# A list schedule that counts TensorE's instructions, and layer-3 parts added on VectorE and GpSimd

## The chip, the cores and the metric

The kernel runs on one core of a Trainium2 chip. The metric is the device time of one execution in microseconds (us), lower is better; the time of a kernel is the median of its runs. Besides its times each kernel has one profiled execution, with a page that sums it up and a trace that can be asked for groups of instructions, waits, the clock that TensorE was granted, and the order in time.

The engines are called PE (TensorE's matrix products; PEld is its loading of weights), DVE (VectorE), ACT (ScalarE), POOL (GpSimd) and SP (SyncE, which only issues DMAs here).

## The reference: what is computed

A decoder of four layers on 32 sequences of 64 tokens, that is 2048 tokens of 256 float32 numbers. Every layer adds three things to the residual `x`: an attention, a cross-attention to a context of 64 vectors of 128 numbers, and a feed-forward part. Each works on the layer norm of `x`.

```python
x = x + _L0_attn_ref(_layernorm(x, axis=-1), ...)
x = x + _L0_xattn_ref(_layernorm(x, axis=-1), ctx_1024, mask_BxS2_bf1, ...)
x = x + _L0_ffn_ref(_layernorm(x, axis=-1), ...)
...
x = x + _L3_ffn_ref(_layernorm(x, axis=-1), ...)
return x
```

Two places matter here. Layer 0's attention has 32 query heads of 64 numbers, 8 key heads, rotary positions and a causal mask: many score products of 64 by 64. Layer 3's feed-forward sends each token to the best 6 of 64 experts (each takes at most 128 tokens), multiplies what the expert returns by the token's weight and adds the six:

```python
h_r = jax.nn.silu(g_r) * v_r
out_r = jnp.einsum('ech,ehd->ecd', h_r, w_down)
y_ts = out_r[flat_e, pos_c]
y_ts = jnp.where(valid[:, None], y_ts, 0.0)
routed = (y_ts.reshape(N, TOPK, C) * w[:, :, None]).sum(axis=1)
```

## The kernel before

**Tiles and stages.** The tokens are 16 tiles of 128; the residual of each, `self.X[i]`, stays in SBUF. `GROUPS = (8, 6, 2)`: the tiles go through the network in three groups. `body` (L2569) writes down the later, narrow stages of one group together with the early, wide stages of the next; `weave` (L2557) takes steps from two such streams by their stated shares.

**Recording.** No engine is called directly. `Recorder` (L380) keeps every operation as an `Op` with the engines that may do it, the views that it reads and writes, and the operations that must come before it. `combine` gives an elementwise operation to DVE or POOL, `either` to DVE or ACT; with `quick` set, as it is for the last stretch of the kernel, `combine` leaves DVE alone.

**Planning.** `in_turns` (L773) makes a list schedule. `Order.run` (L613) keeps a clock for every engine and goes on taking the operation with the lowest key among those whose predecessors are planned: the key is the time at which it could start, with additions. `duration` (L467) says how long each operation is held to take. On TensorE a product's key is raised by `SWITCH` (0.1) when its `part` of the 128x128 array (how many rows and columns it uses, in steps of 32, 64 and 128) is not that of the product before. A tile's buffer is one of a few slots of its tag; it becomes free, by the plan, when the last operation that uses the tile is done. `fill` (L589) puts products without use (`spare`, L874) where PE would wait over 1.6 us. `elsewhere` (L602) leaves an operation to another engine when that one would be done with it sooner. After a plan, `backwards` and `renumber` (L727) turn the list round, with the planned ends as its new order, and plan again: nine plans in all, of which every other one, in the forward direction, may be kept; the shortest by its own clock is. `issue` (L2480) then emits the operations in that order, so nearly every instruction of the profile has line L2504. They are told apart by the tiles they write and read.

**Layer 0's scores.** For one tile `unit_L0_attn` (L1022) makes 128 products of 32 rows (the half of a head, for the rotary positions) by 64 columns by 64, recorded so that the row strip `j` changes after every two:

```python
for half in range(2):
    for j in range(4):
        r = slice(32 * j, 32 * j + 32)
        for x in range(2):
            nc.tensor.matmul(sc[j][64 * x : 64 * x + 64, col],
                qs[hi][r, gp, half, b, x], kk[r, half, hi, b], start=(half == 0), stop=(half == 1))
```

**The end of the kernel.** For the first 14 tiles layer 3's experts work on slots of tokens: `unit_L3_experts` (L2416) makes the products of four experts, weighs the rows, and scatters them with 64 indirect DMAs on POOL's queue into a tensor `parts` in device memory, six rows for each token. `unit_L3_parts` (L2462) loads them again for each tile, in two DMAs of four and two rows a token, adds them and writes the result out. PE sums the first four with the identity as weights, DVE adds the two others and both sums to `x`. The last two tiles use all experts densely instead (`unit_L3_dense`, L2384) in the same stretch of time.

Of the kernel before, what the change touches and what calls it, by code (L numbers as in the profile page):

```python
# [23 lines left out]
ALU = mybir.AluOpType  # L24
# [204 lines left out]
class Tile:  # L229
    def __init__(self, tag, shape, dtype, name, pool):  # L230
        self.tag, self.shape, self.dtype, self.name, self.pool = tag, shape, dtype, name, pool
        self.psum = pool == "psum"
        self.writes, self.reads = [], []
        self.left, self.first, self.last = 0, None, None
        self.slot = self.real = None


class View:
# [282 lines left out]
NEAR = 10  # L521


def combines(op, engine, method):

    if engine == "gpsimd":
        return method == "tensor_tensor" and ALU.pow not in op.args
    return engine == "vector" and not any(v.t.psum for v in op.outs + op.ins if isinstance(v, View))


class Order:
    ENGINES = ("tensor", "vector", "scalar", "gpsimd", "sync")

    def __init__(self, ops, slots, horizon, spare):
        self.ops, self.slots, self.horizon, self.spare = ops, slots, horizon, spare
        self.free_at = {e: 0.0 for e in self.ENGINES}
        self.table, self.moved = 0, 0.0
        self.part = None

        self.until = {"vector": 0.0, "gpsimd": 0.0}  # L540

        self.free = {tag: [(0.0, k) for k in range(n)] for tag, n in slots.items()}

        events = {tag: [] for tag in slots}
        for o in ops:
            for t in o.tiles:
                if t.tag in slots and t.first == o.at:
                    events[t.tag].append((o.at, 0, t))
                if t.tag in slots and t.last == o.at:
                    events[t.tag].append((o.at, 1, t))  # L550
        self.events = {tag: sorted(ev, key=lambda e: e[:2]) for tag, ev in events.items()}

        work, self.pos = 0.0, []
        for o in ops:
            self.pos.append(work)
            if o.ways[0][0] == "tensor":
                work += duration("tensor", o.ways[0][1], o.args, o.kw)
# [55 lines left out]
    def run(self):  # L613
# [6 lines left out]
        for o in self.ops:  # L620
            if o.waits == 0:
                enter(o)
        done, oldest, result, self.ends = [False] * len(self.ops), 0, [], {}
        while not all(done[oldest:]):
            limit = self.pos[oldest] + self.horizon
            best = None
            for e in self.ENGINES:
                now, seen, first = self.free_at[e], 0, 1e9
                for o in ready[e]:
                    if self.pos[o.at] > limit or seen == 32:  # L630
                        break
                    seen += 1
                    since = o.ready
                    opens = [t for t in o.tiles if t.slot is None and t.tag in self.slots]
                    if opens:
                        if any(not self.free[t.tag] for t in opens):
                            continue
                        since = max([since] + [self.free[t.tag][0][0] for t in opens])
                    start = max(now, since)
                    method = next(m for w, m in o.ways if w == e)  # L640
                    cost = duration(e, method, o.args, o.kw)
                    key = max(now, o.soft, since)
                    if e == "tensor":
                        if start == now:
                            first = min(first, self.pos[o.at])
                        if part(method, o.args) != self.part:
                            key += SWITCH
                            cost += SWITCH
                        elif self.pos[o.at] > first + NEAR:
                            key += SWITCH  # L650
                        elif self.part != (128, 128):
                            key = start
                    if e == "scalar":
                        table = TABLES.get(getattr(o.args[2], "name", "") if method == "activation" else "", 0)
                        if table and table != self.table:
                            key += 1.3
                            cost += 1.3
                    if e == "vector" and self.until["gpsimd"] > start and combines(o, e, method):
                        cost += min((1 - BESIDE) * (self.until["gpsimd"] - start), cost / BESIDE - cost)
                    if len(o.ways) > 1 and self.elsewhere(o, e, since, start + cost):  # L660
                        continue
                    if best is not None and (key, o.at) >= best[0] and not (
                        o is best[1] and start + cost < best[3] + best[4]
                    ):
                        continue
                    if opens and not self.may_open(o):
                        continue
                    best = ((key, o.at), o, e, start, cost, opens)
                    if key <= now:
                        break  # L670
            assert best is not None, "nothing can go on"
            _, o, e, start, cost, opens = best
            filler = self.fill(o, start) if e == "tensor" else None
            if filler:
                o, start, opens = filler, self.free_at[e], []
# [20 lines left out]
                table = TABLES.get(getattr(o.args[2], "name", "") if m == "activation" else "", 0)  # L696
                self.table = table or self.table
            if e == "tensor":
                self.part = part(o.ways[0][1], o.args)
            lat = latency(e, o)  # L700
            if o.ways[0][1] in DMA:
                v = next(v for v in o.outs + o.ins if isinstance(v, View) and v.dtype != I32)
# [1 line left out]
                lat = 2.0 + self.moved - got  # L704
            for t in o.tiles:
                t.left -= 1
                if t.left == 0 and t.tag in self.slots:
                    bisect.insort(self.free[t.tag], (got + lat, t.slot))
            for n in o.after:
                same = len(n.ways) == 1 and n.ways[0][0] == e and o.ways[0][1] not in DMA  # L710
                at = (start if e in ("tensor", "sync") else got + 0.03) if same else got + lat
# [3 lines left out]
                if n.waits == 0:  # L715
                    enter(n)
            if not filler:
                done[o.at], self.ends[o] = True, got
            while oldest < len(done) and done[oldest]:
                oldest += 1  # L720
            oldest = min(oldest, len(done) - 1)
# [2 lines left out]
        return result  # L724


def renumber(ops, ends):  # L727

    waits, late = {o: 0 for o in ops}, []
    for o in ops:  # L730
        for n in o.after:
            waits[n] += 1
    count = len(ops)
    for at, o in enumerate(ops):
        if waits[o] == 0:
            heapq.heappush(late, (-ends[o], at, o))
    ops.clear()
    while late:
        o = heapq.heappop(late)[2]
        o.at = len(ops)  # L740
        ops.append(o)
        for n in o.after:
            waits[n] -= 1
            if waits[n] == 0:
                count += 1
                heapq.heappush(late, (-ends[n], count, n))


def rewind(ops):

    for o in ops:
        o.waits, o.ready, o.soft = 0, 0.0, 0.0
        for t in o.tiles:
            t.slot, t.left, t.first, t.last = None, 0, None, None
    for o in ops:
        for n in o.after:
            n.waits += 1
        for t in o.tiles:
            t.left += 1
            t.first, t.last = o.at if t.first is None else t.first, o.at  # L760
# [12 lines left out]
def in_turns(ops, slots, horizon, spare, rounds):  # L773

    best, ops = None, list(ops)
    for k in range(2 * rounds + 1):
        plan = Order(ops, slots, horizon, spare)
        result = plan.run()
        if k % 2 == 0 and (best is None or plan.length < best[0]):
            best = plan.length, result, {t: t.slot for o, _ in result for t in o.tiles}  # L780
        if k < 2 * rounds:
            backwards(ops)
            renumber(ops, plan.ends)
            rewind(ops)
    for t, slot in best[2].items():
        t.slot = slot
    return best[1]


class Net:  # L790
# [1671 lines left out]
    def unit_L3_parts(self, i):  # L2462
        nc = self.nc
        z = [self.b4(4, 256), self.b2(2, 256)]
        for a, (k, m) in enumerate(((0, 4), (4, 2))):
            self.load(
                z[a],
                self.parts(
                    of=lambda x, k=k, m=m: x.rearrange("(t k) n -> t k n", k=6)[i * P : (i + 1) * P, k : k + m, :]
                ),  # L2470
            )
        ps = self.mm()[:, :256]
        self.prod(ps, [(self.k("ident"), z[0][:, k, :]) for k in range(4)])
        nc.combine(z[1][:, 0, :], z[1][:, 0, :], z[1][:, 1, :], ALU.add)
        nc.vector.tensor_tensor(self.X[i], self.X[i], z[1][:, 0, :], ALU.add)
        self.outproj(i, ps)
        nc.sync.dma_start(out=self.out[i * P : (i + 1) * P, :], in_=self.X[i])


# [133 lines left out]
```

## Time and profile before

| | |
|---|---|
| times of three runs | 2928.95, 2929.83, 2934.93 us; median 2929.83 |
| profiled execution | 2933.83 us, span of its instructions 2932.0 us |
| mean granted clock of TensorE | 0.977 |
| PE busy | 2861.3 us, 98% of the span, 28774 records |
| DVE, ACT, POOL busy | 71%, 47%, 49% |
| DMA | 259.22 MB, mean 88 GB/s |
| first parts load, end of the last output | 2881.4 us, 2932 us |

Instructions are called records in the trace. A float32 product is two records of PE, each with a weight load of its own; a transpose is one. The duration of a PE record reaches to the modelled end of its way through the array, which overlaps with the next, so what a product costs in a row of products is the distance of starts. In the lines of groups, "32*64" are the rows and columns of the array that are used, then come what is written, the count, the busy time, the mean duration in ns, and the idle time of the engine before these instructions with what ended it. "issue" means that the engine waited for nothing that the profile shows. In the lines of windows, each engine has its busy time and number of instructions, and after them stand the granted clock (1.00 is full speed), the share of the DMA engines and GB/s.

### The profile page before, as it was taken

How to read it: one execution, taken by the hardware profiler on the slowest of the kernel's cores; microseconds unless marked ns; L12 is line 12 of the kernel's file. 1: busy time of each engine (PE TensorE's matmuls, PEld its weight loads, DVE VectorE, ACT ScalarE, POOL GpSimd, SP SyncE). 2: the span in 40 equal slices, each digit the busy share in tenths (PEclk: the TensorE clock that was granted, in tenths of full speed). 3: DMA queues.
4: the chain of work that ended last, by engine and by line, in shares of the span. 5: the costliest groups of instructions: out<-in, count | busy, mean ns of one | idle time of the engine just before them, and what ended most of it. 6: DMA issues, size and time to landing. Idle time of an engine off the chain costs nothing.

```text
span 2932.0 us, 70600 instructions
## 1 busy us (share of the span) xinstructions
PE 2861.3 (98%) x28774; PEld 2388.2 (81%) x28774; DVE 2080.8 (71%) x5093; ACT 1390.0 (47%) x2637; POOL 1449.5 (49%) x1294
## 2 busy tenths in 40 slices
PE   9999999999999999999999999999999999998899
PEld 8888888777788889888888788878897878877678
DVE  5564447677566656676689997787757889888864
ACT  1223225555544233454466575665335665457360
POOL 4552233223656443423667446677534477357462
PEclk8999999999999899999999999999999999999999
DMA  4002331300161135312100110112473131211245
GB/s 175 22 10 100 117 123 54 142 1 30 62 275 46 59 132 160 124 41 66 55 30 20 44 59 13 45 35 80 134 276 141 57 121 59 75 60 41 89 152 210
DMA packets 120327, 259.22 MB, mean 88 GB/s; under 512 B 27077, under 2 KB 81880, under 8 KB 107588
## 3 DMA queue, kind: packets, MB, share of 16 engines
q1 hardware_dynamic: 110212, 230.61, 22.5%
q0 software_dynamic: 9792, 24.10, 2.4%
q8 instruction: 228, 3.74, 0.5%
q14 instruction: 95, 0.78, 0.1%
HBM read 179.31 MB, written 78.77 MB: 88 GB/s over the span
## 4 chain that ended last, share of the span: by engine, by line
PE 88%; DVE 7%; ACT 2%; POOL 2%; issue 1%; DMA 0%; DVEq 0%; SPq 0%; ACTq 0%; POOLq 0%
PE L_xattn_mm L2504 13%; PE ssm_heads_mm L2504 11%; PE L_attn_mm L2504 10%; PE pair_mm L2504 10%; PE cross_out_mm L2504 9%; PE L_ffn_mm L2504 5%; PE rope_mm L2504 5%; PE L_block_mm L2504 4%; PE turn_mm L2504 3%; PE cross_scores_mm L2504 2%; PE L_dense_mm L2504 2%; PE heads_mm L2504 2%; PE small_scores_mm L2504 1%; PE L_experts_mm L2504 1%; PE norm_mm L2504 1%
## 5 line engine op out<-in xcount | busy, mean ns | idle before, releaser
L2504 PE MATMUL pair_mm<-norm_b,load_ssm_w 128*128 128x256 f32 x1280 | 311.2, 385 | 2.8 <-DVE ssm_heads_b L2504 2.6
L2504 PEld LDWEIGHTS pair_mm<-norm_b,load_ssm_w 128*128 128x128 f32 x1280 | 237.8, 192 | 44.5 <-issue 12.9
L2504 POOL TENSOR_TENSOR L_xattn_sm<-L_xattn_sm,__init___consts 128x8 f32<-128x8 f32 (+2 forms) x64 | 188.2, 2945 | 57.3 <-DVE L_xattn_sm L2504 56.6
L2504 ACT ACT_TABLE_LOAD x154 | 197.6, 1283 | 29.0 <-DVE ssm_heads_b L2504 12.4
L2504 DVE SCALAR_TENSOR_TENSOR ssm_heads_b<-pair_mm,load_ssm_wp,ssm_heads_b 128x248 f32<-128x248 f32 (+2 forms) x480 | 194.3, 465 | 13.3 <-ACT ssm_heads_b L2504 12.5
L2504 POOL TENSOR_TENSOR norm_sm<-norm_sm,__init___consts 128x1 f32<-128x1 f32 (+1 forms) x149 | 95.3, 644 | 199.5 <-DVE norm_sm L2504 184.0
L2504 ACT COPY L_xattn_b<-L_xattn_mm 128x512 f32<-128x512 f32 x176 | 103.1, 591 | 174.3 <-PE L_xattn_mm L2504 160.0
L2504 ACT COPY turn_b<-turn_mm 128x512 f32<-128x512 f32 x203 | 110.7, 593 | 135.5 <-PE turn_mm L2504 134.3
L2504 PE MATMUL rope_mm<-norm_b,load_L_attn_w 128*128 128x128 f32 x1280 | 165.1, 282 | 0.3 <-ACT norm_b L2504 0.2
L2504 PEld LDWEIGHTS rope_mm<-norm_b,load_L_attn_w 128*128 128x128 f32 x1280 | 157.0, 197 | 9.7 <-issue 6.3
L2504 PE MATMUL ssm_heads_mm<-load_ssm_w,ssm_heads_b 128*128 128x256 f32 x640 | 163.5, 385 | 1.3 <-ACT ssm_heads_b L2504 0.8
L2504 ACT COPY norm_b<-norm_mm 128x256 f32<-128x256 f32 (+1 forms) x138 | 58.0, 431 | 189.4 <-PE norm_mm L2504 164.2
L2504 POOL TENSOR_TENSOR L_attn_b<-rope_b 128x256 f32<-128x256 f32 x151 | 109.6, 747 | 71.5 <-DVE rope_b L2504 58.9
L2504 PEld LDWEIGHTS ssm_heads_mm<-load_ssm_w,ssm_heads_b 128*128 128x128 f32 x640 | 115.6, 190 | 32.4 <-issue 18.8
L2504 POOL TENSOR_TENSOR ssm_heads_b<-ssm_heads_b,ssm_heads_b 128x1024 f32<-128x1024 f32 x32 | 76.4, 2387 | 125.5 <-DVE ssm_heads_b L2504 60.9
L2504 DVE TENSOR_TENSOR rope_b<-rope_mm,__init___consts 128x512 f32<-128x512 f32 x160 | 103.2, 680 | 48.0 <-PE rope_mm L2504 37.8
L2504 POOL TENSOR_TENSOR heads_b<-heads_b,heads_sm 128x1024 f32<-128x1024 f32 x53 | 102.1, 1940 | 69.8 <-DVE heads_sm L2504 62.8
L2504 DVE TENSOR_SCALAR norm_b<-__init___x,norm_sm,norm_sm 128x256 f32<-128x256 f32 x192 | 115.8, 620 | 22.7 <-POOL norm_sm L2504 13.4
L2504 PEld LDWEIGHTS L_xattn_mm<-norm_b,load_L_xattn_w 128*128 128x128 f32 x1024 | 119.8, 192 | 7.9 <-issue 4.9
L2504 PE MATMUL L_attn_mm<-load_L_attn_w,L_attn_b 128*128 128x256 f32 x512 | 124.8, 391 | 0.0
L2504 PE MATMUL L_xattn_mm<-norm_b,load_L_xattn_w 128*128 128x128 f32 x1024 | 123.9, 276 | 0.0
L2504 PE MATMUL cross_out_mm<-load_L_xattn_w,cross_out_b 128*128 128x256 f32 x512 | 123.2, 387 | 0.0
(428 smaller groups left out, 7700.5 us busy)
## 6 DMA issues: line engine op xcount, KB each, us to landing
L_block_w<-in_f_rows SPq DMA_DIRECT2D x42, 770.0 KB
queue<-far_w SPq DMA_DIRECT2D x14, 1024.0 KB
load_ssm_w<-in_s_in SPq DMA_DIRECT2D x12, 1024.0 KB
parts<-far_w SPq DMA_DIRECT2D x10, 1024.0 KB
slots<-far_w SPq DMA_DIRECT2D x16, 548.0 KB
L_experts_b<-slots SPq DMA_DIRECT2D x32, 274.0 KB
units_L_xattn_w<-kept_x SPq DMA_DIRECT2D x8, 1024.0 KB
L_parts_b<-parts SPq DMA_DIRECT2D x14, 512.0 KB
```

The costliest lines, as they stand in the source:

```text
L2504: done = getattr(getattr(nc, e), method)(*map(real, op.args), **kw)
```

## The change

On TensorE the planner now keeps a stock of instructions. `STOCK`, `RATE` and `LOW` are 300 instructions, 85 a us, and 150. A product takes 4 from the stock, a transpose 2, and 85 come back in each planned us up to 300. A product that is shorter than its instructions take to come (under 47 ns for 4) gets a higher key when the stock is under 150, by the time that is missing to 150; so a large product that can start is taken first. When the stock doesn't reach for a product, its start is put off. Three smaller things change in the planner: a slot becomes free at the latest end of all operations on its tile, and not at the end of the one that is planned last; when nothing can be chosen, a second try ignores `elsewhere`; `renumber` orders by planned starts and by place in the plan, not by ends. In layer 3's parts PE has no product any more: four additions, each for DVE or POOL as the planner decides, sum the six rows of a token and add them to `x`.

```diff
@@ class Tile
+        self.until = 0.0
@@
+STOCK, RATE, LOW = 300.0, 85.0, 150.0
@@ class Order, __init__
+        self.stock, self.at = STOCK, 0.0
@@ Order.run
-        done, oldest, result, self.ends = [False] * len(self.ops), 0, [], {}
+        stuck, done, oldest, result, self.starts = False, [False] * len(self.ops), 0, [], {}
...
                         elif self.part != (128, 128):
                             key = start
+                        n = 2 if method == "transpose" else 4
+                        stock = min(STOCK, self.stock + (start - self.at) * RATE)
+                        if n > duration(e, method, o.args, o.kw) * RATE:
+                            key += max(0.0, LOW - stock) / RATE
+                        start += max(0.0, n - stock) / RATE
...
-                    if len(o.ways) > 1 and self.elsewhere(o, e, since, start + cost):
+                    if len(o.ways) > 1 and not stuck and self.elsewhere(o, e, since, start + cost):
                         continue
...
+            if best is None and not stuck:
+                stuck = True
+                continue
             assert best is not None, "nothing can go on"
+            stuck = False
...
             if e == "tensor":
-                self.part = part(o.ways[0][1], o.args)
+                self.part, n = part(o.ways[0][1], o.args), 2 if m == "transpose" else 4
+                self.stock, self.at = min(STOCK, self.stock + (start - self.at) * RATE) - n, start
...
+                t.until = max(t.until, got + lat)
                 if t.left == 0 and t.tag in self.slots:
-                    bisect.insort(self.free[t.tag], (got + lat, t.slot))
+                    bisect.insort(self.free[t.tag], (t.until, t.slot))
...
-                done[o.at], self.ends[o] = True, got
+                done[o.at], self.starts[o] = True, (start, len(result))
@@ renumber
-def renumber(ops, ends):
+def renumber(ops, starts):
...
+    key = lambda o: (-starts[o][0], -starts[o][1], o)
...
-            heapq.heappush(late, (-ends[o], at, o))
+            heapq.heappush(late, key(o))
@@ unit_L3_parts
+        add = lambda *v: nc.add([("vector", "tensor_tensor"), ("gpsimd", "tensor_tensor")], (*v, ALU.add), {})
...
-        ps = self.mm()[:, :256]
-        self.prod(ps, [(self.k("ident"), z[0][:, k, :]) for k in range(4)])
-        nc.combine(z[1][:, 0, :], z[1][:, 0, :], z[1][:, 1, :], ALU.add)
-        nc.vector.tensor_tensor(self.X[i], self.X[i], z[1][:, 0, :], ALU.add)
-        self.outproj(i, ps)
+        add(z[0][:, :2], z[0][:, :2], z[0][:, 2:])
+        add(z[1], z[1], z[0][:, :2])
+        add(z[1][:, 0, :], z[1][:, 0, :], z[1][:, 1, :])
+        add(self.X[i], self.X[i], z[1][:, 0, :])
         nc.sync.dma_start(out=self.out[i * P : (i + 1) * P, :], in_=self.X[i])
```

More of the change, by code (lines that the diff above doesn't have):

```diff
@@ L732, in renumber @@
             waits[n] += 1
-    count = len(ops)
-    for at, o in enumerate(ops):
+    key = lambda o: (-starts[o][0], -starts[o][1], o)
+    for o in ops:
         if waits[o] == 0:
-            heapq.heappush(late, (-ends[o], at, o))
+            heapq.heappush(late, key(o))
     ops.clear()
@@ L744, in renumber @@
             if waits[n] == 0:
-                count += 1
-                heapq.heappush(late, (-ends[n], count, n))
+                heapq.heappush(late, key(n))
 def rewind(ops):
@@ L753, in rewind @@
         for t in o.tiles:
-            t.slot, t.left, t.first, t.last = None, 0, None, None
+            t.slot, t.left, t.first, t.last, t.until = None, 0, None, None, 0.0
     for o in ops:
@@ L782, in in_turns @@
             backwards(ops)
-            renumber(ops, plan.ends)
+            renumber(ops, plan.starts)
             rewind(ops)
```

## The prediction

> **What bounds the kernel now.** First the page: how long, which engine, and what ended last.
>
> ```profile
> span 2932.0 us, 70600 instructions
> ...
> PE 2861.3 (98%) x28774; PEld 2388.2 (81%) x28774; DVE 2080.8 (71%) x5093; ACT 1390.0 (47%) x2637; POOL 1449.5 (49%) x1294
> ...
> q8 instruction: 228, 3.74, 0.5%
> ...
> PE 88%; DVE 7%; ACT 2%; POOL 2%; issue 1%; DMA 0%; DVEq 0%; SPq 0%; ACTq 0%; POOLq 0%
> ```
>
> TensorE (PE) is busy 98% and holds 88% of the chain. Only 2932.0 - 2861.3 = 70.7 us lie between its products. But "busy" counts slow products too, so I looked at the clock by stage, in the windows view (the column after POOL is the granted clock).
>
> ```profile
> 0.00:250.00 250.00, 240.45 (x3459) 212.46 (x3460) 139.56 (x245) 64.69 (x115) 121.44 (x126) 0.95 0.20 74
> 1000.00:1250.00 250.00, 242.19 (x2781) 217.41 (x2780) 163.05 (x383) 88.50 (x166) 104.05 (x105) 0.92 0.39 126
> 2000.00:2250.00 250.00, 244.22 (x2391) 211.93 (x2388) 168.20 (x490) 107.26 (x219) 128.13 (x132) 0.97 0.51 178
> ```
>
> These three stretches hold layer 0's attention for the three groups of tiles. Clock lost: 250 x (0.05 + 0.08 + 0.03) = 40 us. The same view for that stage's tile `L_attn_mm` alone (no POOL column, so the clock is after ACT) shows where:
>
> ```profile
> 38.60:41.40 2.80, 2.80 (x102) 2.80 (x104) 0.69 (x1) 0.00 (x0) 1.00 0.01 3
> 41.40:56.70 15.30, 15.30 (x417) 15.21 (x412) 2.80 (x5) 0.00 (x0) 0.50 0.01 3
> 144.50:146.80 2.30, 2.30 (x222) 2.30 (x225) 0.00 (x0) 0.26 (x1) 1.00 0.04 11
> 1036.80:1041.50 4.70, 4.68 (x172) 4.68 (x174) 1.38 (x2) 0.00 (x0) 1.00 0.14 41
> 1041.50:1045.80 4.30, 4.30 (x92) 4.23 (x87) 0.69 (x1) 0.00 (x0) 0.50 0.01 4
> ```
>
> A float32 product leaves two records. So a run of 32x64 products makes one per 2 x 2.80/102 = 55 ns; after 2.8 to 4.7 us of it the clock falls to half, though PE never stops, and one takes 73 to 93 ns. The run at 144.5 goes at 21 ns a product: there the order changes strip of the array from one product to the next, while in the others pair after pair uses the same 32 rows. The timeline shows how that fast run ends:
>
> ```profile
> 143.92 0.60 PE L2504 MATMUL norm_mm<-__init___consts,norm_b 128*128 128x128 f32 x4
> 144.45 2.63 PE L2504 MATMUL L_attn_mm<-L_attn_b,L_attn_b 32*64 32x64 f32 x226
> 148.83 0.48 PE L2504 MATMUL L_attn_mm<-L_attn_b,L_attn_b 32*64 32x64 f32 x30 [1.75 <-issue]
> ```
>
> 226 records are 452 PE instructions with their weight loads; then PE stands 1.75 us for "issue", no engine being waited for. q8 moves 3.74 MB in 228 packets for PE's 57,548 records: 16.4 KB or some 252 instructions a packet. So three costs sit on these runs: a stall when instructions run out, a slow clock, and one strip used at a time.
>
> ```profile
> L2504 PE MATMUL L_attn_mm<-L_attn_b,L_attn_b 32*64 32x64 f32 x4096 | 98.9, 242 | 13.5 <-issue 12.3 <-DVE norm_sm L2504 0.9 <-DVE L_ffn_b L2504 0.2
> L2504 PE MATMUL L_parts_mm<-L_parts_b,__init___consts 128*128 128x256 f32 x112 | 25.6, 380 | 0.0
> ```
>
> (Groups of PE by form: busy, mean ns, idle before and its releaser.)
>
> **The change part by part.** Counts are from the order of instructions of the two kernels.
>
> 1. *Identity products of the parts go*: 14 tiles x 4 = 56 products (112 records). Back to back, 40 of these records took 8.80 us in the timeline at 2912, ends included; two records per product and 216 ns between starts give 432 ns. 56 x 0.432 = **-24.2 us** of PE.
>
> 2. *Their adds*: 28 DVE adds of 256 columns become 15 on DVE (8 of 512 columns, 7 of 256) and 41 on POOL (20 of 512, 21 of 256), and DVE's 14 additions of the product go too. POOL rows: 128x512 1286 ns, 128x256 739 ns; 20 x 1.29 + 21 x 0.74 = 41.3 us. All of them stand behind the 64 scatters on POOL's queue, none between, so they delay no scatter; the last scatter starts at 2878.7, 53.3 us before the end. A load lands 2.4 us after its issue, so POOL needs some 3 + 41 + 3 (last output) = 47 us of those 53. The loads, 14 x 768 KB = 10.75 MB at the 264 GB/s that the stretch 2870 to 2900 shows, take 41 us. PE after the last expert product: 135 products x 0.432 = 58 us before; now 190, of which 114 dense ones make 49 us and the small rest some 10. So the tail keeps its length and starts earlier; the 24 us are had, with about 5 us of cover. I charge **+3** (0 to +24).
>
> 3. *More changes of tile shape*: 627 become 731. Four transposes at 109 ns from 143.92 end at 144.36; the small run starts at 144.45, 0.09 us late. 104 x 0.093 = **+9.7 us**.
>
> 4. *Less running side by side*: neighbours on different row strips fall from 704 to 604 (32x64) and 489 to 389 (64x64). Each lost neighbour takes two products from 21 to 55 ns: 200 x 2 x 0.034 = **+13.6** (0, if those runs stood still afterwards anyway; 27 at twice that).
>
> 5. *Stock of instructions*: instructions beyond the 300th of an unbroken run of small products fall from 3332 to 804. The 12.3 us of "issue" go: **-12.3** (0 to -29, the chain's 1%). [...]
>
> 6. *Clock*: the longest run of 32x64 products falls from 256 to 77, most are 59 = 3.2 us at 55 ns, with large products between. That is within the 2.8 to 4.7 us after which the clock fell, so some falls stay. Of 40 us I take two thirds, **-26** (0 to -40). [...]
>
> 7. *Nothing by themselves*: 6 more filler products (52 to 58) stand in planned waits; 3 fewer ACT table loads, ACT being 47% busy; the slot rule, the second try and the new numbering only reorder. SP's 665 and POOL's 204 DMAs are the same in number. But every engine's order is new, so PE's waits for others are drawn again: 70.7 - 12.5 = 58 us now. I take 0, ends -29 and +29.
>
> Sum: -24.2 + 3 + 9.7 + 13.6 - 12.3 - 26 = -36 us. The profiled execution took 2933.83 us (span 2932.0, 1.8 around it); that is 4 above the median 2929.83 of the three runs. I apply the sum to both: 2898 profiled, **2894** in the median.
>
> **Rivals.**
>
> *The mixing costs and does not pay (slower).* Large products between the bursts run at half clock as well, if the clock still falls: then term 6 is nothing, or a loss. With term 6 at 0, term 5 at 0 and term 4 at 27: -24 + 3 + 9.7 + 27 = +16, **2946**. For it: a burst of 3.2 us is as long as the shortest run that lost the clock. Against: the 15.30 us at half clock came from one run of 256, and none is left. It decides once terms 5 and 6 return less than about 2 us with term 4 at its low end, 16 us with it at its high end. 16%.
>
> *The tail does not follow.* POOL's 41 us of adds run beside DVE's, and take half as long again (62 us > 53); then the 24 us of PE are lost to the adds: -36 + 21 = -15, **2915**. For: the adds become the last work in DVE's and POOL's order. Against: their inputs come at 264 GB/s over 41 us anyhow. 20%.
>
> *The new order does as much harm in waits as it does good*: term 7 at its upper end, -36 + 29 = -7, **2923** to 2936: no change, within 0.2% (6 us, about what a measurement of this kernel can tell). That the change does not mix at all is excluded by the order. 9%.
>
> **How the numbers follow.** The sum's case, 55%, holds 2856 (terms 5, 6 and 7 each half way to their good ends, -38) to 2912. The range takes in the rivals up to 2942, and leaves out most of the slow one's far half. Faster by over 0.2%: 55 + 20 = 75%, and 1 of the third rival's 9; same 8%; slower 16%.
>
> **What would show it.** Right: clock 0.97 or better in the attention stretches; "issue" gone from PE's waits; bursts of 118 records with large products between; no `L_parts_mm`; last expert product some 30 us earlier and the end about 60 us behind it. Wrong: half clock in the same stretches; POOL busy to the last microsecond with PE long done (second rival); PE's waits for DVE, ACT and POOL well over 58 us (third).

## The result, and the profile after

The changed kernel is slower. Seven runs have a median of 2945.71 us beside 2926.0 us of seven runs of the kernel before: ratio 1.0059, 95% interval 1.0046 to 1.0072. The forecast was 2894, faster, and the top of its range was 2942. The profiled execution took 2938.70 us (span 2936.9); that of before took 2933.83, so the two traces differ by 5 us and the medians by 20. The traces show where things moved; sizes below go by ratios. The changed kernel's trace is of the fastest of its seven runs.

The page of the changed kernel, the same lines as before:

```profile
span 2936.9 us, 70435 instructions
...
PE 2865.2 (98%) x28674; PEld 2381.3 (81%) x28674; DVE 2098.6 (71%) x5092; ACT 1373.9 (47%) x2607; POOL 1500.2 (51%) x1336
...
PE 87%; DVE 8%; ACT 2%; issue 2%; POOL 1%; DMA 0%; POOLq 0%; SPq 0%; ACTq 0%; DVEq 0%
```

One hundred records fewer on PE, 51 us more on POOL, and a chain that is still PE's. Only the windows show the change (after POOL: granted clock, DMA share, GB/s). The first three are those of the prediction, the fourth is the end of the kernel, and the last is that end in the kernel before:

```profile
0.00:250.00 250.00, 246.13 (x3271) 212.10 (x3272) 135.28 (x238) 59.26 (x106) 112.55 (x120) 0.94 0.21 76
...
1000.00:1250.00 250.00, 249.99 (x2944) 221.39 (x2941) 175.16 (x391) 103.80 (x186) 115.04 (x113) 0.98 0.38 125
...
2000.00:2250.00 250.00, 244.89 (x2421) 212.63 (x2421) 165.00 (x486) 97.30 (x206) 133.95 (x137) 0.96 0.51 176
...
2750.00:2937.00 187.00, 158.41 (x1555) 125.22 (x1553) 114.90 (x376) 75.65 (x152) 117.17 (x117) 0.89 0.49 163
...
2750.00:2937.00 187.00, 169.83 (x1649) 138.86 (x1648) 111.40 (x397) 73.52 (x148) 75.74 (x76) 0.97 0.48 164
```

The clock rose in the middle stretch alone (0.92 to 0.98), and 250 x (0.06 + 0.02 + 0.04) = 30 us are still lost where 40 were. At the end PE is busy 158 us at 0.89; before it was 170, at 0.97. The group of the small score products:

```profile
L2520 PE MATMUL L_attn_mm<-L_attn_b,L_attn_b 32*64 32x64 f32 x4096 | 105.2, 232 | 1.9 <-issue 1.9
```

The stall put down to issue fell from 12.3 to 1.9 us, as forecast; but the products themselves rose from 98.9 to 105.2.

Then the end. PE's last product ended at 2916.7, before at 2928.5; the kernel ended 20.1 us behind it, before 3.6. The windows of the additions alone (tile `L_parts_b`; columns DVE, POOL, clock, DMA share, GB/s):

```profile
2880.00:2890.00 10.00, 2.57 (x4) 6.68 (x6) 0.85 0.35 123
2890.00:2900.00 10.00, 0.00 (x0) 10.00 (x11) 0.98 0.59 198
2900.00:2910.00 10.00, 0.00 (x0) 6.32 (x7) 1.00 0.34 106
2910.00:2920.00 10.00, 4.59 (x7) 7.85 (x8) 1.00 0.50 157
2920.00:2930.00 10.00, 4.72 (x5) 7.95 (x9) 0.55 0.23 79
```

POOL adds to the last (2928.0) and yet has holes; DVE's share comes at the end. POOL's waits say why:

```profile
POOL __init___x L2520 <- DVE L_parts_b L2520: 19.7, 4, 12.1
POOL L_parts_b L2520 <- DMA L_parts_b<-parts: 5.4, 1, 5.4
```

(Waiter and what it waited for: us in all, times, longest.) The four additions of a tile are a chain, and the planner gave its links to both engines. DVE's links stood behind DVE's work for the last two tiles (`L_dense_b`, which waited 23.5 us for ACT and PE), and POOL stood behind DVE. The loads were late too: the last of the 28 was issued 50 us after the first (2861.8 to 2911.6; before 26 us). SyncE issues them in one order with the outputs, and its longest waits from the first load on were these:

```profile
SPq L2520 <- PE L_dense_mm L2520: 22.3, 9, 9.7
SPq L2520 <- POOL __init___x L2520: 18.1, 8, 9.7
```

So the loads stood 22.3 us for PE's products of the last two tiles, whose tiles have the same slots (tag `b2`), and once 9.7 us behind an output that POOL's chain held. For an addition's buffer they waited under 1 us.

POOL's last addition isn't the end either. Each engine closes with an instruction DRAIN; here are those of the changed kernel (POOL, SP) and of the kernel before (POOL), with the shortest, median and longest duration in ns, the first start and the last:

```profile
L2625 POOLq DRAIN  x3: 40/107/9412, 2926.6 to 2936.6; - x3
L2625 SPq DRAIN  x3: 7/7/7, 2930.5 to 2936.3; - x3
L2609 POOLq DRAIN  x3: 40/107/14177, 2873.5 to 2931.8; - x3
```

POOL's longest DRAIN, its first, ends at 2926.64 + 9.41 = 2936.05, 8.1 us behind POOL's last addition. In the kernel before POOL was done at 2879.6 and its close was over at 2887.7, again 8.1 us later, but long before the end. In the changed kernel the last output has landed at 2929.7 and SP is through at 2930.6; the program then stands 5.4 us for POOL. Of the 20.1 us behind PE, 11.2 go to the additions and 8.9 to the close.

**Where it happened.** I laid the products that both kernels share on one scale (each counted by its columns and its share of the array) and read off when a given share of this work was reached. In us, minus is earlier than before, for profiled executions; e1 to b1 are experiments explained below. The weights are a choice: by columns alone the 95% row has -4.7 for the changed kernel and +2.1 for e1, while the entries with the order kept stay. In p1 and b1 PE's last products are fillers without use; the last useful ones end 8 us earlier.

| share of TensorE's work | changed | e1 planner | e2 parts | m1 mixing, order kept | p1 parts, order kept | b1 all, order kept |
|---|---|---|---|---|---|---|
| 20% | +8.0 | +6.6 | -12.4 | -11.2 | -3.6 | -16.3 |
| 55% | -9.6 | -16.9 | -14.5 | -18.2 | -6.5 | -27.7 |
| 75% | +5.0 | -1.9 | -5.4 | -7.0 | -6.3 | -34.5 |
| 95% | +5.5 | -0.5 | -13.4 | -6.9 | -4.1 | -36.5 |
| last product | -11.7 | +2.2 | -20.7 | -6.9 | -22.2 | -54.5 |
| from PE's end to the end (before 3.6) | 20.1 | 3.9 | 23.8 | 3.6 | 24.3 | 24.2 |

p1 has the order of before up to the last two rows: its -4 to -6.5 is the scatter between two executions of one order. The changed kernel scatters as much: a second trace of it (a1, at its median) has PE's last product 5.5 us later, 6.2 us earlier than before, and the same 20.1 us behind it.

### The profile page after: what moved, and what is told of

The parts are those of the page before. It is cut to its first block, busy times and chain, and to the rows that moved or that the text cites. A ratio compares the mean times of both kernels' runs of the same rounds, so it can differ in the third digit from the quotient of the medians.

```text
span 2936.9 us, 70435 instructions
## 1 busy us (share of the span) xinstructions
PE 2865.2 (98%) x28674; PEld 2381.3 (81%) x28674; DVE 2098.6 (71%) x5092; ACT 1373.9 (47%) x2607; POOL 1500.2 (51%) x1336
## 4 chain that ended last, share of the span: by engine, by line
PE 87%; DVE 8%; ACT 2%; issue 2%; POOL 1%; DMA 0%; POOLq 0%; SPq 0%; ACTq 0%; DVEq 0%
PE L_xattn_mm L2520 13%; PE ssm_heads_mm L2520 10%; PE L_attn_mm L2520 10%; PE pair_mm L2520 10%; PE cross_out_mm L2520 9%; PE rope_mm L2520 5%; PE L_ffn_mm L2520 5%; PE L_block_mm L2520 4%; PE turn_mm L2520 3%; PE cross_scores_mm L2520 2%; PE L_dense_mm L2520 2%; PE heads_mm L2520 2%; PE small_scores_mm L2520 2%; PE L_experts_mm L2520 1%; PE L_expert_mm L2520 1%
## 5 line engine op out<-in xcount | busy, mean ns | idle before, releaser
L2520 DVE SCALAR_TENSOR_TENSOR ssm_heads_b<-pair_mm,load_ssm_wp,ssm_heads_b 128x252 f32<-128x252 f32 (+2 forms) x480 | 193.7, 465 | 24.3 <-ACT ssm_heads_b L2520 17.4
L2520 PE MATMUL rope_mm<-norm_b,load_L_attn_w 128*128 128x128 f32 x1280 | 172.5, 287 | 0.4 <-ACT norm_b L2520 0.2
L2520 ACT COPY L_xattn_b<-L_xattn_mm 128x512 f32<-128x512 f32 x164 | 96.6, 590 | 144.2 <-PE L_xattn_mm L2520 132.8
L2520 POOL TENSOR_TENSOR ssm_heads_b<-ssm_heads_b,ssm_heads_b 128x1024 f32<-128x1024 f32 x34 | 83.0, 2444 | 136.8 <-DVE ssm_heads_b L2520 105.7
L2520 ACT ACTIVATE ssm_heads_b<-ssm_heads_b 128x512 f32<-128x512 f32 (+1 forms) x120 | 91.7, 772 | 72.0 <-DVE ssm_heads_b L2520 41.0
L2520 PEld LDWEIGHTS L_xattn_mm<-norm_b,units_L_xattn_w 128*128 128x128 f32 x1024 | 119.3, 192 | 4.6 <-issue 2.4
```

Source lines behind the costliest of these rows:

```text
L2520: done = getattr(getattr(nc, e), method)(*map(real, op.args), **kw)
```

## The experiments

Theory after the result: the end doesn't follow (the second rival), and the mixing is about neutral. Rival: the mixing costs (the first rival, whose 2946 is the measured time). All ratios are to the kernel before on the same chip. On the chips of c1, c2, x1, x2 and of h1, h2, c3, c4 the kernel before itself took 3046 us; those runs are compared with it there.

### Each half alone, planned anew: e1, e2

e1 is the changed planner with the old `unit_L3_parts`; e2 the old planner with the new one (and the second try, without which its plan gets stuck):

```diff
 e1, in after:  unit_L3_parts as in before (four identity products, DVE adds)
 e2, in before: unit_L3_parts as in after, and
-                    if len(o.ways) > 1 and self.elsewhere(o, e, since, start + cost):
+                    if len(o.ways) > 1 and not stuck and self.elsewhere(o, e, since, start + cost):
```

> The changed planner with the old layer-3 parts (identity products on TensorE, adds on DVE). Kernel before: 2926; changed kernel: 2946. Theory 1, the end of the kernel doesn't follow: the mixing itself is about neutral (at 95% of the common products the changed kernel was 1.5 us behind), the loss is the 20 us tail behind PE's last product. Then this kernel is within 8 us of before, 2918 to 2934, with a tail of about 4 us. Theory 2, the mixing costs more than it returns: this kernel is 10 to 20 us slower than before, 2936 to 2946, whatever its tail.

> The old planner (with the second try only, which changes no plan that doesn't get stuck) and the new layer-3 parts: 20 adds on DVE, 36 on POOL by its choice. Theory 1: PE loses 24 us of products, the end behind PE's last product grows by about 17, so 7 us faster, 2914 to 2924, and the tail is 15 to 20 us long. Theory 2: the parts edit gives its 24 us, 2900 to 2906, with a tail below 6 us.

Measured: e1 1.0035 (1.0023 to 1.0047), e2 1.0033 (1.0021 to 1.0045). Both are slower by 10 us, and 0.35 + 0.33 = 0.68% is the whole (0.59). e1 fits the second theory, though only just, and e2 neither: its PE ended 20.7 us earlier, the end 23.8 us behind it. By these two the parts bring nothing and the planner costs something. But each is a new plan.

### The additions moved, the preference off: e3, e4

```diff
 e3, in body:
-    issue(tc, in_turns(...), Net.SLOTS)
+    order = in_turns(...)
+    issue(tc, [(o, "vector" if o in net.nc.adds else e) for o, e in order], Net.SLOTS)
 e4:
-STOCK, RATE, LOW = 300.0, 85.0, 150.0
+STOCK, RATE, LOW = 300.0, 85.0, 0.0
```

(`adds` holds the 56 new additions.)

> The changed kernel with its order kept as it is, only the 41 adds that POOL has are given to DVE at the same places of the order. Theory 1, POOL's slow adds (1.26 us for 512 columns) hold the buffers of the loads and so the tail: 28 adds of 512 and 28 of 256 columns take DVE about 28 x 0.68 + 28 x 0.4 = 30 us instead of 50, the tail behind PE's last product falls from 20 to about 6 us, time 2946 - 14 = 2932 (2926 to 2937). Rival, the loads themselves (10.75 MB at about 260 GB/s, 41 us) or TensorE's end hold the tail: 2942 to 2950.

> The changed kernel with LOW at 0: small products get no higher key, so runs of up to 256 are back, while the other planner changes and the new parts stay. Theory 1, mixing is about neutral: within 8 us of the changed kernel, 2938 to 2952, with the tail of 15 to 20 us. Theory 2, the mixing costs: 10 to 20 us faster than the changed kernel, 2926 to 2936, and the lost clock in the attention stretches back at 40 us.

Measured: e3 1.0020 (1.0006 to 1.0034), 11 us better than the changed kernel (1.0059) with nothing but 41 additions on another engine; the end came 13.3 us behind PE, not 6. Of the 6.8 us that the tail lost, 5.1 are POOL's close: from the last addition to the end 3.8 us instead of 8.9. The additions themselves end 1.7 us sooner behind PE. So POOL's part in the end is real, but less by its slow additions (medians of 1.27 us for 512 columns and 0.72 for 256 in the changed kernel; DVE's here 0.68 and 0.42) than by ending last. e4 1.0003 (0.9990 to 1.0016): without the preference 16 us better, with the long tail (20.1 us) still there. That is what the rival asked for, if the two plans may be compared; its other sign didn't come, the clock lost in the three attention stretches was 32 us and not 40 again.

### What a new plan is worth by itself: c1 to c4, a1

```diff
-SWITCH = 0.1
+SWITCH = 0.101
```

c1 and c3 are before with this line, c2 and c4 the changed kernel with it. a1 is the changed kernel once more.

> Control: the kernel before with SWITCH 0.101 instead of 0.1. No cost of the chip changes by that, but the planner draws another order (nearly every row of every engine moves). If a new order by itself moves the time by 10 us or so, the 10 us of the first two experiments can't be put down to their edits. Theory 1: within 12 us of before, either sign, with a tail of about 4 us. Rival, the old order was a lucky one that any other draw loses: 8 to 20 us slower.

> Control: the changed kernel with SWITCH 0.101. Theory 1, a draw is worth about 10 us and the tail some 17: within 10 us of the changed kernel, 2937 to 2957 on the scale where before is 2928, with a tail of 15 to 22 us. Rival, the changed kernel's order was an unlucky draw: 2915 to 2932.

> The kernel of c1 once more (SWITCH 0.101, the planner of before): it was 1.0% faster than before on a chip where before takes 3046 us. If the draw is better by itself: 0.988 to 0.995. If the gain belongs to that chip: 0.997 to 1.005.

> The kernel of c2 once more (the changed kernel with SWITCH 0.101): 0.43% slower than before on the other chip. Theory, the changed kernel is slower in any draw by its tail, with about 10 us either way by the draw: 1.001 to 1.009, with a tail of 20 us behind PE's last product.

> The changed kernel itself, for a comparison on the same chip as the other three: ratio 1.003 to 1.008 as before. If the chip matters more than the edit (the kernel before took 3046 us on the chip of the second call), it can come out elsewhere.

Measured: c1 0.9897 (0.9881 to 0.9914), c3 0.9910 (0.9895 to 0.9925); c2 1.0043 (1.0029 to 1.0056), c4 1.0060 (1.0047 to 1.0074); a1 1.0054 (1.0040 to 1.0068). I had expected 12 us at most. A change of 1% in a constant that says nothing new of the chip gave 0.9 to 1.0%, 27 to 31 us. Both c1 and c3 ran where the kernel before took 4% more, and no such run was made on the other chips. Where the gain arose can be read on the scale of the table (by columns alone). At 90% of the work c1 and c3 stand 37 and 44 us behind the trace of before, h1, which has the order of before on such a chip, 40. At 95% they stand 28 and 36 us behind, h1 60. So they gained in the stretch of the expert products, where these chips lose time (last section), and what a draw is worth on the others isn't shown. It is enough for doubt: e1's 10 us and e4's 16 can't safely be put down to an edit. From here on I kept the plan of before and changed the list behind it.

### Mixing without a new plan: m1

```diff
+    for o, e in order:          # behind the plan of before
...
+        low = need(o) > take(o) * 85.0 and stock < 150.0
+        while low and stock < 240.0:
+            ways = (n for n in todo[todo.index(o):][:300] if need(n) < take(n) * 85.0 and can(n, starts[o]))
+            n = next(ways, None)
...
+            emit(n, e)
```

`can`: its inputs end, by the plan, before `o` starts, and its buffer is free.

> The kernel before with its plan kept; behind it, where a small product stands while the stock (300, 85 a us, 4 a product) is under 150, large products that the plan has ready are taken forward until it is 240. So the mixing alone, without a new draw: the longest run of 32x64 products falls from 256 to 98, runs over 60 from 14 to 4, changes of shape rise from 627 to 683, neighbours on other strips stay (826 of 832). Terms 5 and 6 of the prediction against 56 x 0.093 = 5 us of changes: ratio to before 0.987 to 0.995. Mixing neutral: 0.997 to 1.002. Rival, mixing costs: 1.004 to 1.008.

Measured: 0.9987 (0.9976 to 0.9997), 4 us faster. Neither the forecast's 0.987 to 0.995 nor the rival's 1.004 to 1.008: the mixing is about neutral. Its group of score products:

```profile
L2566 PE MATMUL L_attn_mm<-L_attn_b,L_attn_b 32*64 32x64 f32 x4096 | 98.1, 233 | 2.0 <-issue 1.2 <-DVE norm_sm L2566 0.9
```

The stall fell from 12.3 to 1.2 us. The table shows 18 us gained by 55% of the work and 11 of them given back between 70 and 75%, in the third group's attention. Windows of `L_attn_mm` there in m1 (PE, PEld, DVE, ACT, clock, DMA share, GB/s):

```profile
2085.90:2089.30 3.40, 2.35 (x28) 1.77 (x32) 0.00 (x0) 0.00 (x0) 0.50 1.00 398
2089.30:2092.70 3.40, 3.40 (x66) 2.70 (x60) 0.00 (x0) 1.07 (x2) 0.50 0.48 129
2092.70:2096.10 3.40, 1.77 (x58) 1.58 (x54) 0.00 (x0) 0.00 (x0) 0.50 0.27 89
2096.10:2099.50 3.40, 2.56 (x46) 2.56 (x46) 0.00 (x0) 0.00 (x0) 0.50 0.38 115
```

and the same products in the kernel before:

```profile
2096.20:2099.60 3.40, 2.08 (x44) 1.36 (x40) 0.00 (x0) 0.00 (x0) 1.00 1.01 406
2099.60:2103.10 3.50, 3.26 (x142) 3.15 (x140) 0.00 (x0) 1.07 (x2) 0.99 0.77 248
2103.10:2106.50 3.40, 1.32 (x24) 1.13 (x20) 0.00 (x0) 0.00 (x0) 0.50 0.30 96
```

Before, the clock fell when the run was nearly over: 186 records went through 6.9 us at 0.99 to 1.00, and 24 through the 3.4 us at 0.50 behind them. In m1 it had fallen by 2085.9, and the 198 records of these rows crawled through 13.6 us at half speed. So here the same work cost little or much by where the fall landed. In the traces of before and of the changed kernel every half-speed stretch within the span lasts 3.41 us or a whole multiple of it (3.4 to 20.5 us before, 3.4 to 23.9 after), but for the one that the changed kernel's end cuts off. What brings a fall about isn't shown.

### The parts without a new plan: p1, h1, h3

The products are dropped behind the plan; where DVE added their sum, an engine makes three additions.

```diff
+            if op in net.dropped:                # the four identity products
+                continue
+            for v in net.instead.get(op, ()):    # z0[:2] += z0[2:];  z0[0] += z0[1];  x += z0[0]
...
+                getattr(nc, e).tensor_tensor(*map(real, v), ALU.add)
 p1: all 14 tiles on DVE.  h1: odd tiles only, even ones keep their products.
 h3: tiles 1, 4, 7, 10, 13 wholly on POOL, the others on DVE.
```

> The kernel before with its plan kept; the 56 identity products are left out behind it and, where DVE added their sum to x, DVE makes three adds (512, 256, 256 columns) instead of one. PE loses 24 us, DVE gets 14 x 1.1 = 15 us more, POOL nothing. Theory, the end follows when POOL has no adds: the last load lands at about 2911, some 5 us of adds and outputs behind it, 10 to 16 us faster, ratio 0.9945 to 0.9965, tail behind PE's last product 8 to 14 us. Rival, loads and adds take all of it whoever adds: 0.998 to 1.002. Rival, all 24 us are had: 0.992.

> The kernel before with its plan kept; as in p1 DVE adds the parts, but only for the seven odd tiles, the seven even ones keep their products. In p1 DVE stood without a gap from 2892.8 to 2927.1 in adds while PE had ended at 2906. Theory, the end is bound by whoever adds and the two engines must share: PE ends 12 us earlier than before, DVE has 7 x 1.26 + 7 x 2.4 = 26 us instead of 34, both end near 2918 to 2920: 8 to 12 us faster, ratio 0.996 to 0.9975. Rival, something behind both (loads, outputs) ends at 2927 whatever adds: 0.999 to 1.001.

> As p1 (plan of the kernel before kept, no products for the parts), but five of the fourteen tiles are added by POOL, which has nothing to do there, and nine by DVE. In p1 DVE's adds ran back to back for 34 us and ended 21 us after PE. Theory, the end is bound by the adder's own time: DVE 9 x 2.45 = 22 us, POOL 5 x 4.2 = 21 us, slowed by each other to 25 to 30: end 4 to 9 us earlier than p1, ratio to before 0.997 to 0.9985. Rival, POOL beside DVE takes back what it carries: 0.9995 to 1.003.

Measured: p1 1.0000 (0.9991 to 1.0010), h1 1.0000 (0.9988 to 1.0012), h3 1.0016 (1.0003 to 1.0028). None gained. p1's windows behind its last scatter (PE, PEld, DVE, ACT, POOL, clock, DMA share, GB/s):

```profile
2886.00:2896.00 10.00, 9.64 (x44) 7.88 (x43) 4.28 (x11) 1.15 (x3) 0.00 (x0) 1.00 1.03 399
2896.00:2906.00 10.00, 5.43 (x22) 4.02 (x20) 9.60 (x23) 0.00 (x0) 0.00 (x0) 0.92 1.05 393
2906.00:2916.00 10.00, 0.27 (x1) 0.00 (x0) 9.58 (x23) 0.00 (x0) 0.00 (x0) 0.50 0.42 150
2916.00:2926.00 10.00, 0.00 (x0) 0.00 (x0) 9.59 (x22) 0.00 (x0) 0.00 (x0) 0.50 0.16 52
```

PE is done at 2906, the DMAs thin out, and DVE adds without a gap to 2927: 14 x (0.68 + 4 x 0.42) = 33 us of additions that start only at 2893, though loads were issued from 2877 on: in the order they stand behind DVE's part of the last two tiles, for which DVE waited 15.3 us for ACT. The end is where it was, with another engine in it. h1 should have split this; its DVE waited for the same dense work until 3013 (of that run's 3043 us), then added without a gap to 3036, and PE, whose filler had stood 4.7 us for DVE, made the last four products from 3034.3 on. A better order would be needed, and wasn't tried. h3 shows why POOL is no help. From its timeline (start, us, engine, what):

```profile
2912.72 0.78 POOL L2518 TENSOR_TENSOR __init___x<-__init___x,L_parts_b 128x256 f32<-128x256 f32 x1
2912.96 0.83 DVE L2506 TENSOR_TENSOR __init___x<-__init___x,L_parts_b 128x256 f32<-128x256 f32 x1
...
2915.23 0.83 DVE L2518 TENSOR_TENSOR __init___x<-__init___x,L_parts_b 128x256 f32<-128x256 f32 x1
2915.86 0.79 POOL L2506 TENSOR_TENSOR __init___x<-__init___x,L_parts_b 128x256 f32<-128x256 f32 x1
...
2917.68 0.42 DVE L2506 TENSOR_TENSOR __init___x<-__init___x,L_parts_b 128x256 f32<-128x256 f32 x1
2918.03 0.42 DVE L2518 TENSOR_TENSOR L_parts_b<-L_parts_b 128x256 f32<-128x256 f32 x1
```

As long as POOL adds, DVE's addition of 256 columns to `x` takes 0.83 us; POOL's last ends at 2916.6, and it takes 0.42. From 2891.6 to 2916.6 POOL finished five tiles and DVE some five: in those 25 us DVE alone, at p1's 2.4 us a tile, does ten. POOL gave nothing. (Its close, if it ends 8.1 us behind its last addition as in the changed kernel, was over at 2924.7 and cost nothing: DVE added to 2927.4.) Why the two slow each other isn't shown.

### What the array's strips are worth: x1, x2, b1, h2, b2

```diff
+            while 128 not in k and o in starts:   # k: rows and columns that o uses
+                ways = [n for n in todo[todo.index(o):][:64] if shape(n) == k
+                        and (n is o or age(n) < age(o) and can(n, starts[o]))]
+                n = min(ways, key=age)            # its part of the array was used longest ago
...
+                emit(n, e)
 x1: behind the plan of before.  x2: behind the plan of the changed kernel.
 b1: x1 + m1 + p1.  h2: x1 + m1 + h1.  b2: x1 + m1 + h3.
```

> The kernel before with its plan kept, but behind the plan each small product (32 or 64 rows by up to 64 columns) may be replaced by one that the plan has ready and whose rows and columns of the array were used longest ago. The 32x64 products with 64 columns took 53 ns apiece on the mean, 21 ns in the run at 144.5 where strips alternate; the four small groups together took 251 us. Theory: one strip used at a time is a real cost and TensorE's order decides it, 2048 products from 53 to 21-30 ns and some 20 us of the others, 50 to 90 us faster, 2838 to 2878, and fewer stretches at half clock. Rival: the products wait for their inputs or for instructions anyway, the runs stand still instead: 2905 to 2930, with more idle time of PE by issue or by DVE.

> The same rearrangement behind the changed kernel's plan. Theory that the stock of instructions is worth counting once small products run fast: this gains more than x1 does, time 2825 to 2865 though its base is 17 us slower, and issue waits are smaller than in x1. Rival, mixing has nothing to give: the same gain as x1, so that this stays 10 to 20 us slower than x1.

> The kernel before with its plan kept and all three behind it: small products alternated over the array as in x1, mixed as in m1, parts added by DVE as in p1. If the gains add up: 1.1% of x1 and 0.4% of p1, ratio 0.980 to 0.988. If instructions hold the faster small runs, mixing adds to that, 0.975. Rival, the stages in which x1 lost its gain again (behind 2000 us) hold it: 0.990 to 0.995.

> As b1 (alternated, mixed, plan of the kernel before kept) with half of the parts by products as in h1. b1 had a tail of 24 us behind PE's last product, all of it DVE's adds. Theory as in h1: 8 to 12 us less than b1, ratio 0.985 to 0.987. Rival: as b1, 0.989.

> As b1 (alternated and mixed, 0.9894), with the parts shared as in h3. Theory: 4 to 9 us less than b1, ratio 0.986 to 0.988. Rival: 0.989 to 0.992.

Measured: x1 0.9889 (0.9872 to 0.9906), x2 0.9862 (0.9844 to 0.9879), b1 0.9894 (0.9878 to 0.9910), h2 0.9886 (0.9868 to 0.9903), b2 0.9895 (0.9876 to 0.9914). b1 takes 2898.8 us: 31 less than before, 46 less than the changed kernel on the same chip. As m1 gives 4 and p1 nothing, nearly all of it is put down to the alternation, which didn't run by itself on that chip; the tails stay (24 us in b1, 20 in b2). The score products in b1, then in x1 and x2:

```profile
L2588 PE MATMUL L_attn_mm<-L_attn_b,L_attn_b 32*64 32x64 f32 x4096 | 67.4, 235 | 13.7 <-issue 11.8 <-DVE norm_sm L2588 0.9 <-DVE L_ffn_b L2588 0.4
```

```profile
L2564 PE MATMUL L_attn_mm<-L_attn_b,L_attn_b 32*64 32x64 f32 x4096 | 72.4, 245 | 38.7 <-issue 34.2 <-DVE L_route_sm L2564 2.6 <-DVE norm_sm L2564 0.9
```

```profile
L2580 PE MATMUL L_attn_mm<-L_attn_b,L_attn_b 32*64 32x64 f32 x4096 | 75.2, 233 | 13.7 <-issue 12.2 <-DVE rope_b L2580 0.7 <-POOL L_attn_b L2580 0.4
```

Busy falls from 98.9 to 67.4, and the four groups of small products with the most records go from 251 to 214 us, start to start: the gain is where the edit was, so that a mere draw is unlikely. I had hoped for 50 to 90 us; the 32x64 records with 256 columns stayed at 50 us between starts, and part of the rest went to the stall: x1, unmixed, stands 34.2 us for issue, x2, mixed, 12.2, and b1 11.8. That mixing shortens this stall is shown. That it gives time isn't: the intervals of x1 and x2 overlap, and b1 (0.9894) is no better than x1 (0.9889).

## Why the prediction was wrong

Parts (terms 1 and 2) were to give 21 us and gave none; planner (terms 3 to 7) was to give 15 and cost 10, of which the experiments can call only the mixing. The prediction's own sign shows where: the last expert product some 30 us earlier, the end about 60 us behind it. It came 25 us earlier (2869.8 to 2844.5), and the end 92 us behind it, before 62.

| term | forecast | what the runs showed |
|---|---|---|
| 1 identity products | -24.2 | right as far as PE goes: it ends 22 us earlier in p1, 18 of them in this step (last product against 95%) |
| 2 their additions | +3 (0 to +24) | **the step that failed**: +24 with the order kept (p1), some +29 with POOL (h3, 1.0016); the changed kernel has 5.4 of POOL's close besides |
| 3 changes of shape | +9.7 | the price held: ahead of a change the next start is 203 ns behind a 128x128 record instead of 111, 309 behind a 128x256 one instead of 216 (medians, before) |
| 4 neighbours on other strips | +13.6 (0 to 27) | the four small groups, start to start: 251 to 263 us though 10 us of stall left them, so about +22; slow clock and 4 us more of waits for other engines are in it |
| 5 stock | -12.3 | about right: 12.3 to 1.9 us of issue; m1 12.3 to 1.2. That a stock of instructions runs out, and its 300 and 85 a us, are the author's estimate: no run shows them |
| 6 clock | -26 (0 to -40) | **failed**: half of the half-speed stretches is 66.6 us before and 69.3 after, of which 7.9 fall behind PE's last product and cost nothing: -5; m1 -14 |
| 7 waits | 0 | PE's waits without issue 52 to 48 us |

*Term 2.* The forecast had "POOL needs some 3 + 41 + 3 = 47 us of those 53", "with about 5 us of cover". The price was right: POOL's additions took 43 us. What it missed: each tile is one chain over two engines, so POOL waited 19.7 us for links of DVE that stood behind DVE's dense work; SyncE's queue stood 22.3 us for PE's dense products before it could issue loads; POOL's close comes 8.1 us behind its last addition; and DVE's addition of 256 columns takes 0.83 us beside POOL's, alone 0.42. The first three are in the changed kernel's trace, the fourth in h3. (The 2.4 us from issue to landing are those of the scatters; no view of before has them for a load, and m1's page has 8.2 us for the loads of 512 KB.) "So the tail keeps its length" compared PE's products with POOL's queue; the end goes by the slowest engine behind the last scatter, and p1 shows that DVE alone already needs to 2927. In before PE had been adding beside DVE, and POOL was idle.

*Term 6.* I took two thirds because most runs were cut to 3.2 us. But the clock still fell: 17 half-speed stretches before, 19 in the changed kernel up to PE's last product, and m1's fall took most of a run (13.6 us at 0.50). How long a run must be for a fall no run shows. In the changed kernel the end lost some 7 us more of clock than before (0.97 to 0.89 over 187 us is 15, less the 8 behind PE's end); PE had less work there, 158 us for 170. The 40 us were too large a base as well: they count half of every half-speed stretch as lost. The prediction's row of 15.30 us at 0.50 has 417 records, which at its 55 ns a product take 11.5 us at full speed, a loss of 3.8 and not of 7.7. That fits m1, which by the same count has 14 us less of lost clock and 11 less of stall, and is 4 us faster; how the rest of that difference divides isn't known.

*The rivals.* The second had the mechanism, the end that doesn't follow, and about its place: POOL's stretch from first to last addition was 62 us, its number, though by waiting and not by being slow. The first had the time, 2946, by luck as far as m1 shows: mixing alone is 0.13% faster. e4's 16 us speak for it and stay open.

*A sum.* The low end, 2856, takes terms 5, 6 and 7 half way to their good ends as -38; by the ends stated it is -8, -7 and -15, that is -30 and 2864. It played no part.

*Open.* How the planner's +10 us (e1) divides. Mixing is -4 with the order kept; the rest is the new numbering, the slot rule, terms 3 and 4 and the draw of a new order. No run separates them. With the order kept, mixing gives -4 and the parts 0 (p1) to +5 (h3), and POOL's close is 5 more; of the changed kernel's +17 that leaves, as an estimate, some 11 us without a shown cause.

## What to carry to other kernels

Work taken off the busiest engine at the end of a kernel is a gain only if the engine that gets it is free there: list every engine's queue behind the last input, in order, with what each piece waits for, up to its closing instruction. Measure what a second adder gives before the work is shared: in h3 VectorE's addition took 0.83 us beside GpSimd's and 0.42 alone, and sharing gained nothing (1.0016). Count an engine's close too: GpSimd's ended 8.1 us behind its last instruction, and in the changed kernel the program stood 5.4 us for it. Where a planner writes the order, run a control with a meaningless change, on the same chip, before a few tenths of a per cent are put down to an edit, or change the list behind a kept plan. Here small products gained more from being spread over the array (1.1%) than from being mixed with large ones (0.13%).

## What I had not expected of the hardware

- 30 runs of the kernel before on one chip lie between 2922.4 and 2936.7 us, and their times go with the mean granted clock (0.980 for the fastest, 0.975 to 0.976 for the slowest; correlation -0.89, 2.5 us for each 0.001). So the scatter goes with the granted clock; what moves it isn't shown.
- On two chips the kernel before took 3046 us at a clock of 0.956 to 0.961. h1 there was 3 us behind the trace of before at 60% of the work, 10 at 70% and 36 at 75% (by columns alone), and took 151 us from the first to the last expert product instead of 100. The engines' idle time ahead of these experts' instructions that is put down to issue or to another core or an unknown queue was 51 us together, in the trace of before 4. What stands behind it is open.
